# Summing the four corners of a deformable-convolution gather in a PSUM bank, beside layer 1

## The chip, the cores and the metric

One core of a Trainium2 chip runs the whole network in one launch. The metric is the time of one execution in microseconds (us). TensorE is called PE (PEld is its weight load), VectorE DVE, ScalarE ACT, GpSimd POOL, and SP issues DMAs. All data are float32.

## The reference, cut to what matters

Four layers run in sequence on an input of 8 images of 128 channels by 64 x 64; each is `x = x + layer(group_norm(x))`. Three of them matter here.

- Layer 1 propagates along rows and columns. For each of four directions (down, up, right, left), with its own 9-tap 1-D convolution over 128 channels:

```python
def step(prev, cur):
    new = cur + jax.nn.relu(_conv1d(prev, w))
    return (new, new)
_, outs = jax.lax.scan(step, xm[0], xm[1:])
```

  That is a chain of 63 dependent steps per direction, 252 in all.
- Layer 2 is a 5 x 1 convolution, a 3-tap one per channel and a gate.
- Layer 3 is a deformable convolution. An offset convolution gives each pixel and each of the 9 taps a fractional position and a mask; the sample is the weighted sum of the four corners of that position, and a matrix product over taps and channels follows:

```python
samp = corner(y0, x0, (1 - wy1) * (1 - wx1)) + corner(y0, x0 + 1, (1 - wy1) * wx1) \
     + corner(y0 + 1, x0, wy1 * (1 - wx1)) + corner(y0 + 1, x0 + 1, wy1 * wx1)
samp = samp * mask[:, None]
out = jnp.einsum('bckhw,ock->bohw', samp, dcn_w.reshape(COUT, C, KK))
```

Then a batch norm over all images, a leaky rectifier, and the residual.

## The kernel before, in words

Layer 1 keeps its state X in SBUF for four images at a time. Images 0 to 3 pass through it beside the end of layer 0. After an exchange, images 4 to 7 pass through it while layer 2 of images 0 to 3 and layer 3 of images 0 to 2 (and the first 30 ticks of image 3) run. The part of that second passage from tick 96 on is the stage of the change. One step of layer 1 (`propagate`, L930 and L937) is 9 float32 products, which the trace shows as 18 matmuls and 18 weight loads, into one PSUM tile `ps_l`; DVE then applies `X = max(ps_l, 0) + X`, and the next step reads that X.

Layer 2 and the preparation of layer 3 (`Layer2.plan`) are lists of small functions with due ticks, 96 ticks to an image: `t1_product` L1064, `t4_product` L1078, the gate in DVE L1092 to L1100, `tokens` (PE transposes L1134, copied by ACT L1137 and L1140, and stored as a table in DRAM), `offsets` L1161, `offsets_out` (ACT `omc` L1172, then transposes L1175), and the positions and weights of the gather.

Layer 3 (`Layer3`) runs one image behind. A tick handles 3 of the 9 taps for 128 pixels. What it issues at tick n:

1. `fetch`: three indirect DMAs from POOL (L1288), one per tap. Each brings, for 128 pixels, the four corners of 128 channels: 512 columns of `got`, which has 3 x 4 x 128 columns. There are `GOT` = 6 such buffers. After layer 1 has ended, X is cut into more of them.
2. The functions that earlier ticks left for this one: `sum` of tick n-1, `turn` of n-2, `keep` of n-3, and every sixth tick `convolve`, later `bias` and `store`.
3. `weigh`: DVE multiplies corners 0 to 2 of all three taps by their weights in one operation of 1152 columns (L1306), and ACT multiplies corner 3 in three activations of 128 columns (L1310).

With `sums` = 2, beside layer 1, `sum` adds the corners on DVE in two operations (L1321): corners 0 and 1 get 2 and 3 (768 columns), then corner 0 gets corner 1 (384 columns). `turn` transposes the three results on PE into a tile `ps_s` (L1328), of which a pool has three; `keep` copies it to `samp` on ACT (L1335). `convolve` (L1341) multiplies by the weights, 9 products over two pixel groups. With `sums` = 0, after layer 1, nothing is added on DVE: `turn` accumulates the four corners in PSUM with four transposes per tap, and the product's weights lie in the PSUM bank that layer 1 has left (`wps`, L1302).

The order on each engine is the program's order, written out by hand in the loop over ticks n: first the tick of layer 3 (from n = 96), then the functions of layer 2 that are due, then as many steps of layer 1 as a running balance of PE's costs allows (`load`, `pace`, `STEP`). Layer 1 ends at `last` = 414, so 318 ticks run with `sums` = 2. After it the loop interleaves the residual of images 4 to 7 (`residual`, L887 to L897), whose layer 2 comes next.

Of the kernel before, what the change touches and what calls it, by code (L numbers as in the profile page):

```python
# [10 lines left out]
F32 = mybir.dt.float32  # L11
I32 = mybir.dt.int32
AF = mybir.ActivationFunctionType
ALU = mybir.AluOpType
PSUM = bass.MemoryType.PSUM
DRAM = bass.MemoryType.DRAM

P = 128
B, C, H, W = 8, 128, 64, 64
# [4 lines left out]
T = 512  # L24
# [16 lines left out]
def conv_preact_kernel(ctx: ExitStack, tc: tile.TileContext, a: dict, out: bass.AP):  # L41
    nc = tc.nc
# [38 lines left out]
    with tc.tile_pool(name="x", bufs=1) as xp, tc.tile_pool(name="l1w", bufs=1) as wd, tc.tile_pool(  # L81
        name="l1ps", bufs=1, space=PSUM
# [16 lines left out]
        with tc.tile_pool(name="l2w", bufs=1) as wp, tc.tile_pool(name="l2", bufs=2) as w2, tc.tile_pool(  # L99
            name="l3", bufs=2  # L100
        ) as w3, tc.tile_pool(name="l2ps", bufs=2, space=PSUM) as p2, tc.tile_pool(
            name="l3ps", bufs=3, space=PSUM
        ) as p3, tc.manual_schedule():
            st2 = [const.tile([P, NCH, 6], F32, name=f"st2_{b}") for b in range(B)]
            one = propagate(tc, a, wd, pl, X)
# [20 lines left out]
            for b in range(B):  # L126
                for when, what in sorted(two.plan(b).items()):
                    n = b * two.TICKS + when
                    if b == NB2:
                        n = (b + 1) * two.TICKS - (two.TICKS - 5 - when) // 2  # L130
# [3 lines left out]
            first = two.TICKS  # L134
            load = {
                n: 2 + 18 * (n % 6 == 3) + sum(f.products for f in plans.get(n, ())) for n in range(first, last)
            }
            steps, taken, total = 4 * H, 2 * NCH - 1, 0
            for n in range(min(plans), (B + 1) * two.TICKS):
                b, i = n // two.TICKS - 1, n % two.TICKS  # L140
                if b >= 0:
                    three.tick(b, i, two.done[b], 2 if n < last else 0)
                for f in plans.pop(n, ()):
                    f()
                if n < two.TICKS:
                    if n % 3 == 0:
                        next(one)
                        taken += 1
                elif n < last:
                    if n == first:  # L150
                        pace = (sum(load.values()) + STEP * (steps - taken)) / (last - first)
                    total += load[n]
                    while total + STEP / 2 <= pace * (n + 1 - first) and taken < steps:
                        next(one)
                        taken, total = taken + 1, total + STEP
                else:
                    if n == last:
                        run(one)
                        three.bank = pl
                    if n < last + 12 or n % 3 == 0:  # L160
                        if next(late, True) and not three.more:
                            size = 3 * 4 * C
                            flat = X.rearrange("p h b -> p (h b)")
                            for i in range(HW * NB2 // size):
                                piece = flat[:, i * size : (i + 1) * size]
                                three.more.append(piece.rearrange("p (k q c) -> p k q c", k=3, c=C))
                            three.turns = 0
# [1090 lines left out]
class Layer3:  # L1258


    PAIR, G3, WT = 2, 3, 16

    def __init__(self, tc, a, ident, tables, od, st, wp, w2, pp):
        nc = self.nc = tc.nc
        self.ident, self.tables, self.od, self.st = ident, tables, od, st
        self.w2, self.pp = w2, pp
        self.dcn_w = wp.tile([P, KK, P], F32, name="dcn_w")
        nc.sync.dma_start(self.dcn_w, a["dcn_w"])
        self.dcn_b = wp.tile([P, 1], F32, name="dcn_b")
        nc.sync.dma_start(self.dcn_b, a["dcn_b"])  # L1270
        self.bank = self.wps = None
        self.more, self.turns = [], 0
        self.late = {}
        self.n = 0
# [21 lines left out]
    def weigh(self, b, t, k0, wgt, got, sums):  # L1296
        nc, G3 = self.nc, self.G3
        if k0 == 0 and t % self.WT == 0:
            self.wps = None
            if self.bank is not None:  # L1300
                self.wps = self.bank.tile([P, self.WT, KK, 3], F32, tag="ps_l1", name="wps")
                nc.scalar.copy(self.wps, wgt[:, t : t + self.WT, :, 0:3])  # L1302
        if k0 == 0 and t % self.PAIR == 0:
            self.samp = self.w2.tile([P, KK, self.PAIR * P], F32, name="samp")
        w = wgt[:, t, k0 : k0 + G3, 0:3] if self.wps is None else self.wps[:, t % self.WT, k0 : k0 + G3, :]
        nc.vector.tensor_mul(  # L1306
            got[:, :, 0:3, :], got[:, :, 0:3, :], w.unsqueeze(3).to_broadcast([P, G3, 3, C])
        )
        for k in range(G3):
            nc.scalar.activation(  # L1310
                got[:, k, 3, :], got[:, k, 3, :], AF.Identity, scale=wgt[:, t, k0 + k, 3:4]
            )
        self.later(1, self.sum, got, sums)
        self.later(2, self.turn, got, sums, self.samp, k0, t % self.PAIR * P)
        if k0 + G3 == KK and t % self.PAIR == self.PAIR - 1:
            self.later(4, self.convolve, b, t + 1 - self.PAIR, self.samp)

    def sum(self, got, sums):
        for n in range(sums):
            q = 2 - n  # L1320
            self.nc.vector.tensor_add(got[:, :, 0:q, :], got[:, :, 0:q, :], got[:, :, q : 2 * q, :])  # L1321

    def turn(self, got, sums, samp, k0, col):
        nc, parts = self.nc, 4 >> sums
        ps = self.pp.tile([P, self.G3, P], F32, name="ps_s")
        for k in range(self.G3):
            for q in range(parts):
                nc.tensor.matmul(  # L1328
                    ps[:, k, :], lhsT=got[:, k, q, :], rhs=self.ident, is_transpose=True,
                    start=(q == 0), stop=(q == parts - 1),  # L1330
                )
        self.later(1, self.keep, ps, samp, k0, col)
# [123 lines left out]
```

## Time and profile before

| what | value |
|---|---|
| median of 5 runs | 6308.25 us (6293.68 to 6322.04) |
| the profiled execution, time | 6319.36 us |
| its span | 6317.4 us |
| busy over the span | PE 83%, PEld 57%, DVE 67%, ACT 47%, POOL 69% |
| mean granted PE clock | 0.899 |
| first gather issue, last layer-1 update | 2948.08 us, 4393.52 us |
| last gather issue | 6132.5 us |

All groups, waits and chains that the text reads come from the profiled execution. A row of a group names the line, the engine, the operation, the tile written and the tiles read, the shapes and the count; then the busy time and the mean of one, and after the second bar the time the engine stood idle before them, with what ended it. In a timeline, a row gives start and duration, and in brackets the idle time before it with its releaser. "issue" is time in which the engine waited for nothing that the profile shows. Matmul ends are modelled, so a busy PE need not be at its peak. The span cut in 40 slices (each digit the busy share in tenths; the stage of the change lies in slices 19 to 28):

```profile
PE   3677877889999999889999999998888787876650
DVE  4889999888787878232877777776655454544334
ACT  4667677664554543122443444433445455554442
POOL 3777888876666666112777787777667777777765
```

### The profile page before, as it was taken

Reading aid. Unit: us, or ns where it says so; the run is one execution under the profiler, and the core shown is the slowest. Engines: PE = TensorE matmul, PEld = TensorE weight load, DVE = VectorE, ACT = ScalarE, POOL = GpSimd, SP = SyncE. Lnnn points to the kernel's source line nnn. Section 1 sums busy time; section 2 is a strip of 40 time slices with the busy share of each in tenths; the row PEclk is TensorE's granted clock in tenths of the full one; section 3 lists DMA queues with packets and bytes.
Section 4 is the critical chain, followed back from the end, with each engine's and each line's share of the span. In section 5 each row is a group of like instructions: output and inputs, shape, how many; then the busy total and the mean of one; then the engine's idle time right before and its main releaser. Section 6 shows DMA issues by size and latency. Waiting matters only on the chain.

```text
span 6317.4 us, 76412 instructions
## 1 busy us (share of the span) xinstructions
PE 5250.7 (83%) x25372; PEld 3616.2 (57%) x25372; DVE 4217.2 (67%) x4615; ACT 2999.1 (47%) x5848; POOL 4335.4 (69%) x3758
## 2 busy tenths in 40 slices
PE   3677877889999999889999999998888787876650
PEld 1122222247676767666777777787666666665550
DVE  4889999888787878232877777776655454544334
ACT  4667677664554543122443444433445455554442
POOL 3777888876666666112777787777667777777765
PEclk7777777789999999999999999999989899998885
DMA  4676676655555545233776777767788888787778
GB/s 122 194 203 188 194 201 186 182 160 149 144 148 146 151 137 145 69 136 104 214 212 198 212 205 214 215 192 203 253 274 253 248 250 250 244 258 219 216 212 292
DMA packets 516713, 1231.28 MB, mean 195 GB/s; under 512 B 79320, under 2 KB 120224, under 8 KB 514272
## 3 DMA queue, kind: packets, MB, share of 16 engines
q0 software_dynamic: 184320, 604.13, 32.8%
q1 hardware_dynamic: 320480, 597.10, 31.9%
q10 hardware_dynamic: 11520, 25.18, 1.0%
q8 instruction: 202, 3.31, 0.2%
q14 instruction: 191, 1.56, 0.1%
HBM read 1064.79 MB, written 161.32 MB: 194 GB/s over the span
## 4 chain that ended last, share of the span: by engine, by line
PE 52%; DMA 17%; DVE 6%; issue 4%; POOL 4%; ACT 3%; SPq 0%; POOLq 0%; DVEq 0%; ACTq 0%
PE ps_l L930 29%; DMA X<-table,idx 6%; DMA got<-table,idx 6%; PE ps_o L1341 5%; PE ps_s L1328 4%; PE ps_t L1064 3%; POOL got L1288 2%; PE ps_y L801 2%; PE ps_t L1078 2%; PE ps_off L1161 1%; DVE X L937 1%; DMA o_in<-od 1%; DVE hb L786 1%; DVE got L1306 1%; PE ps_x L488 1%
## 5 line engine op out<-in xcount | busy, mean ns | idle before, releaser
L1288 POOL DMA_INDIRECT got<-table,idx x1614 | 1766.7, 1095 | 774.5 <-issue 369.3
L930 PE MATMUL ps_l<-X,w_dir 128*128 128x240 f32 (+4 forms) x9072 | 2031.3, 379 | 93.7 <-DVE X L937 65.8
L930 PEld LDWEIGHTS ps_l<-X,w_dir 128*128 128x128 f32 x9072 | 1704.5, 192 | 466.2 <-DVE X L937 210.2
L792 POOL TENSOR_TENSOR hb<-hb,C 128x1024 f32<-128x1024 f32 x512 | 1209.1, 2362 | 65.3 <-DMA C<-cs 24.1
L786 DVE TENSOR_TENSOR_SCAN hb<-da,carry,ub_ps 128x512 f32<-128x512 f32 x896 | 1097.9, 1267 | 81.3 <-ACT da L769 25.1
L769 ACT ACTIVATE da<-dt_s,a_neg 128x512 f32<-128x512 f32 x1024 | 678.2, 714 | 657.0 <-DVE hb L786 604.4
L1310 ACT ACTIVATE got<-got,wgt 128x128 f32<-128x128 f32 x1614 | 587.1, 402 | 531.8 <-DMA got<-table,idx 503.4
L1288 POOL DMA_INDIRECT X<-table,idx x690 | 653.6, 947 | 210.2 <-issue 91.7
L937 DVE SCALAR_TENSOR_TENSOR X<-ps_l,X 128x256 f32<-128x256 f32 x504 | 213.3, 423 | 776.4 <-PE ps_l L930 773.9
L1328 PE MATMUL ps_s<-ident,got 128*128 128x128 f32 x3594 | 520.7, 293 | 174.1 <-ACT samp L1335 77.8
L777 DVE TENSOR_TENSOR ub_ps<-u_s,B_ps 128x1024 f32<-128x1024 f32 x512 | 625.6, 1222 | 53.7 <-DMA u_s<-ud 28.7
L1306 DVE TENSOR_TENSOR X<-X,wps 128x1152 f32<-128x1152 f32 x230 | 311.3, 1354 | 451.3 <-DMA X<-table,idx 416.0
L1328 PEld LDWEIGHTS ps_s<-ident,got 128*128 128x128 f32 x3594 | 454.6, 152 | 267.1 <-ACT samp L1335 105.7
L1341 PE MATMUL ps_o<-samp,dcn_w 128*128 128x256 f32 x2304 | 530.9, 386 | 0.0
L1306 DVE TENSOR_TENSOR got<-got,wps 128x1152 f32<-128x1152 f32 x202 | 272.6, 1351 | 359.8 <-DMA got<-table,idx 337.8
L1328 PE MATMUL ps_s<-ident,X 128*128 128x128 f32 x2760 | 380.1, 297 | 154.9 <-ACT samp L1335 94.1
L1321 DVE TENSOR_TENSOR got<-got 128x768 f32<-128x768 f32 x636 | 484.7, 762 | 25.0 <-ACT got L1310 6.7
L1341 PEld LDWEIGHTS ps_o<-samp,dcn_w 128*128 128x128 f32 x2304 | 441.8, 195 | 71.8 <-issue 14.8
L1335 ACT COPY samp<-ps_s 128x384 f32<-128x384 f32 x768 | 361.3, 471 | 234.8 <-PE ps_s L1328 234.5
L1306 DVE TENSOR_TENSOR got<-got,wgt 128x1152 f32<-128x1152 f32 x336 | 453.0, 1349 | 28.2 <-DMA got<-table,idx 28.0
L1328 PEld LDWEIGHTS ps_s<-ident,X 128*128 128x128 f32 x2760 | 346.1, 155 | 196.5 <-ACT samp L1335 108.1
L791 POOL COPY carry<-hb 128x2 f32<-128x2 f32 x512 | 95.7, 187 | 527.0 <-DVE hb L786 491.5
(219 smaller groups left out, 5796.8 us busy)
## 6 DMA issues: line engine op xcount, KB each, us to landing
dt_s<-dtd SPq DMA_DIRECT2D x512, 256.0 KB
u_s<-ud SPq DMA_DIRECT2D x512, 256.0 KB
C<-cs SPq DMA_DIRECT2D x128, 256.0 KB
table<-tok SPq DMA_DIRECT2D x128, 256.0 KB
got<-table,idx POOLq DMA_INDIRECT x1614, 3.9
x<-x2d SPq DMA_DIRECT2D x48, 384.0 KB
x3h<-x3d SPq DMA_DIRECT2D x16, 1056.0 KB
dtd<-dt SPq DMA_DIRECT2D x64, 256.0 KB
```

The costliest lines, as they stand in the source:

```text
L769: nc.scalar.activation(da[:, k], steps[i]["dt"], AF.Exp, scale=a_neg[:, q, k : k + 1])
L777: nc.vector.tensor_mul(ub, st["u"].unsqueeze(1).to_broadcast([P, 2, T]), s["B", h])
L786: nc.vector.tensor_tensor_scan(hb[:, k, :], st["da"][:, k, :], ub[:, k, :], start, ALU.mult, ALU.add)
L792: nc.gpsimd.tensor_mul(hb, hb, S[c]["C", h])
L930: nc.tensor.matmul(ps[:, c0:c1, :], lhsT=w[:, k, :], rhs=v[:, prev, c0 + k - PAD : c1 + k - PAD, :], start=(k == PAD), stop=(k == K - 1),)
L1288: nc.gpsimd.indirect_dma_start(out=got[:, k, :, :].rearrange("p q c -> p (q c)"), out_offset=None, in_=self.tables[b], in_offset=bass.Indi ...
L1306: nc.vector.tensor_mul(got[:, :, 0:3, :], got[:, :, 0:3, :], w.unsqueeze(3).to_broadcast([P, G3, 3, C]))
L1310: nc.scalar.activation(got[:, k, 3, :], got[:, k, 3, :], AF.Identity, scale=wgt[:, t, k0 + k, 3:4])
L1321: self.nc.vector.tensor_add(got[:, :, 0:q, :], got[:, :, 0:q, :], got[:, :, q : 2 * q, :])
L1328: nc.tensor.matmul(ps[:, k, :], lhsT=got[:, k, q, :], rhs=self.ident, is_transpose=True, start=(q == 0), stop=(q == parts - 1),)
L1335: self.nc.scalar.copy(samp[:, k0 : k0 + self.G3, col : col + P], ps)
L1341: nc.tensor.matmul(ps, lhsT=self.dcn_w[:, k, :], rhs=samp[:, k, :], start=(k == 0), stop=(k == KK - 1))
```

## The change

Where `sums` is set, that is beside layer 1: the weighted corner 0 goes to a PSUM bank (`banks[2]`, 384 of its 512 columns), corner 1 is weighted in place, both on DVE. ACT weighs corners 2 and 3, six activations instead of three. `sum` adds corners 1 and 2 into the bank and writes bank + corner 3 to corner 0 of `got`: three operations of 384 columns. Transposes use the two other banks in turn. The three tiles `ps_s` become three fixed banks, so PSUM holds no more than before; after layer 1 all three serve the transposes again, and the products, activations and transposes there are what they were. The instructions and the order on POOL stay as they are.

```diff
--- before.py
+++ after.py
@@ -99,7 +99,7 @@
         with tc.tile_pool(name="l2w", bufs=1) as wp, tc.tile_pool(name="l2", bufs=2) as w2, tc.tile_pool(
             name="l3", bufs=2
         ) as w3, tc.tile_pool(name="l2ps", bufs=2, space=PSUM) as p2, tc.tile_pool(
-            name="l3ps", bufs=3, space=PSUM
+            name="l3ps", bufs=1, space=PSUM
         ) as p3, tc.manual_schedule():
             st2 = [const.tile([P, NCH, 6], F32, name=f"st2_{b}") for b in range(B)]
             one = propagate(tc, a, wd, pl, X)
@@ -1268,6 +1268,7 @@
         nc.sync.dma_start(self.dcn_w, a["dcn_w"])
         self.dcn_b = wp.tile([P, 1], F32, name="dcn_b")
         nc.sync.dma_start(self.dcn_b, a["dcn_b"])
+        self.banks = [pp.tile([P, T], F32, name=f"bank{i}") for i in range(3)]
         self.bank = self.wps = None
         self.more, self.turns = [], 0
         self.late = {}
@@ -1302,27 +1303,36 @@
                 nc.scalar.copy(self.wps, wgt[:, t : t + self.WT, :, 0:3])
         if k0 == 0 and t % self.PAIR == 0:
             self.samp = self.w2.tile([P, KK, self.PAIR * P], F32, name="samp")
-        w = wgt[:, t, k0 : k0 + G3, 0:3] if self.wps is None else self.wps[:, t % self.WT, k0 : k0 + G3, :]
-        nc.vector.tensor_mul(
-            got[:, :, 0:3, :], got[:, :, 0:3, :], w.unsqueeze(3).to_broadcast([P, G3, 3, C])
-        )
-        for k in range(G3):
-            nc.scalar.activation(
-                got[:, k, 3, :], got[:, k, 3, :], AF.Identity, scale=wgt[:, t, k0 + k, 3:4]
-            )
+        w = wgt[:, t, k0 : k0 + G3, :] if self.wps is None else self.wps[:, t % self.WT, k0 : k0 + G3, :]
+        spread = lambda q0, q1: w[:, :, q0:q1].unsqueeze(3).to_broadcast([P, G3, q1 - q0, C])
+        if sums:
+            nc.vector.tensor_mul(self.total(), got[:, :, 0, :], w[:, :, 0:1].to_broadcast([P, G3, C]))
+            nc.vector.tensor_mul(got[:, :, 1:2, :], got[:, :, 1:2, :], spread(1, 2))
+        else:
+            nc.vector.tensor_mul(got[:, :, 0:3, :], got[:, :, 0:3, :], spread(0, 3))
+        for q in (2, 3) if sums else (3,):
+            for k in range(G3):
+                nc.scalar.activation(
+                    got[:, k, q, :], got[:, k, q, :], AF.Identity, scale=wgt[:, t, k0 + k, q : q + 1]
+                )
         self.later(1, self.sum, got, sums)
         self.later(2, self.turn, got, sums, self.samp, k0, t % self.PAIR * P)
         if k0 + G3 == KK and t % self.PAIR == self.PAIR - 1:
             self.later(4, self.convolve, b, t + 1 - self.PAIR, self.samp)
 
+    def total(self):
+        return self.banks[2][:, 0 : self.G3 * P].rearrange("p (k c) -> p k c", c=P)
+
     def sum(self, got, sums):
-        for n in range(sums):
-            q = 2 - n
-            self.nc.vector.tensor_add(got[:, :, 0:q, :], got[:, :, 0:q, :], got[:, :, q : 2 * q, :])
+        if sums:
+            total = self.total()
+            for q, to in ((1, total), (2, total), (3, got[:, :, 0, :])):
+                self.nc.vector.tensor_add(to, total, got[:, :, q, :])
 
     def turn(self, got, sums, samp, k0, col):
         nc, parts = self.nc, 4 >> sums
-        ps = self.pp.tile([P, self.G3, P], F32, name="ps_s")
+        ps = self.banks[self.n % (2 if self.bank is None else 3)]
+        ps = ps[:, 0 : self.G3 * P].rearrange("p (k c) -> p k c", c=P)
         for k in range(self.G3):
             for q in range(parts):
                 nc.tensor.matmul(
```

## The prediction

> **What bounds the kernel now.** I read the span in slices first, then the groups of one stretch, then the waits and the chain of work. The change touches only ticks 96 to 413 of the gather, which run beside the second half of layer 1, from about 2960 to 4394 us. The groups of instructions between 3000 and 4390 us, shapes kept apart (count, busy us, mean ns, idle before it and who ended it):
>
> ```profile
> L1288 POOL DMA_INDIRECT got<-table,idx x929 | 1097.5, 1181 | 293.3 <-issue 217.9 <-ACT got L1310 20.7 <-ACT samp L1335 19.6
> L1306 DVE TENSOR_TENSOR got<-got,wgt 128x1152 f32<-128x1152 f32 x311 | 419.7, 1350 | 28.2 <-DMA got<-table,idx 28.0
> L1310 ACT ACTIVATE got<-got,wgt 128x128 f32<-128x128 f32 x932 | 330.3, 402 | 207.7 <-DMA got<-table,idx 196.7 <-DVE got L1321 9.3 <-DVE bn_st L1357 0.3
> L1321 DVE TENSOR_TENSOR got<-got 128x768 f32<-128x768 f32 x311 | 296.2, 952 | 12.3 <-ACT got L1310 5.0
> L1321 DVE TENSOR_TENSOR got<-got 128x384 f32<-128x384 f32 x310 | 177.3, 572 | 10.7
> ```
>
> POOL is saturated: 1097.5 us of gather issues plus 293.3 us before them is the whole 1390 us, and nearly all of those gaps are the 0.30 us that stands before every issue. But PE is nearly full too. In the table of stretches (us, then PE, PEld, DVE, ACT and POOL busy, clock) the stage and the late gather read:
>
> ```profile
> 2960.00:4394.00 1434.00, 1371.33 (x6682) 1104.81 (x6680) 1079.79 (x1379) 571.54 (x1514) 1123.13 (x954) 0.99 0.70 205
> 4670.00:6140.00 1470.00, 1136.37 (x6937) 925.07 (x6936) 669.41 (x645) 720.05 (x1832) 1107.86 (x1167) 0.90 0.80 242
> ```
>
> PE is busy 96% of the stage, so a faster POOL can win only the places where PE stood still for a late gather. The timeline shows them; this is the worst (start, duration, idle before it):
>
> ```profile
> 3549.92 1.36 DVE L1306 TENSOR_TENSOR got<-got,wgt 128x1152 f32<-128x1152 f32 x1 [4.35 <-DMA got<-table,idx]
> ...
> 3552.26 7.08 PE L930 MATMUL ps_l<-X,w_dir 128*128 128x256 f32 x18 [3.64 <-DVE X L937]
> ```
>
> DVE's queue stood on a gather, the layer-1 update X behind it came late, PE waited 3.64 us, and its 18 matmuls then took 7.08 us instead of the usual 4.02.
>
> **Why an issue takes 1181 ns.** After 4800 us, where the product's weights come from PSUM, the same issue takes 947 to 948 ns. Beside layer 1 it is lengthened when it starts during a DVE operation with two SBUF inputs:
>
> ```profile
> 4373.42 1.35 DVE L1306 TENSOR_TENSOR got<-got,wgt 128x1152 f32<-128x1152 f32 x1
> 4374.04 1.55 POOL L1288 DMA_INDIRECT got<-table,idx  x1 [0.30 <-issue]
> 4375.76 0.45 PEld L1328 LDWEIGHTS ps_s<-ident,got 128*128 128x128 f32 x3
> 4375.90 0.94 POOL L1288 DMA_INDIRECT got<-table,idx  x1 [0.30 <-issue]
> ```
>
> The issue at 4374.04 starts while the product runs (to 4374.77) and needs 0.6 us more than the one at 4375.90.
>
> [...]
>
> **The change, part by part** (318 ticks of three gathers each).
>
> *DVE.* Gone per tick: 1350 + 952 + 572 = 2874 ns. Added: two products and three sums of 384 columns. An SBUF sum of 384 takes 572 ns. For PSUM operands the nearest rows are layer 2's gate, 512 columns at 685 and 687 ns; between the 384 and 768 rows (0.99 ns a column) an SBUF sum of 512 would take 699. So PSUM costs nothing extra: 558 to 572 each, 2.79 to 2.86 us, and two more gaps of 35 ns (10.7 us over 310). I take +0.04 us a tick (ends -0.08 and +0.12), 13 us on an engine that is busy 75%; it lies beside PE's matmuls, except where PE waits for a sum (below).
>
> [...]
>
> *POOL.* A tick now has 2.87 us of DVE work with two SBUF inputs; afterwards only the two products have them, 1.14 us (a sum has one input in PSUM). An issue that meets an operation at a random moment waits its remainder, so the excess goes with the sum of squares: 1.350² + 0.952² + 0.572² = 3.06 against 2 x 0.572² = 0.65. The excess of 234 ns becomes 50 ns; its ends are 0 and 234. A tick then needs 3 x (0.947 + 0.050 + 0.305) = 3.9 us of POOL, while the stage gives 1434 / 318 = 4.5. POOL runs ahead until the six buffers stop it.
>
> *ACT.* Three more weighings. Three in a row take 0.99 us, so +315 us: ACT goes from 571 to 886 us of 1434, 62%. Behind them in ACT's queue stand the samples' copy L1335 (which frees a transpose bank for PE), layer 2's copies, and `omc` L1172, for which PE waits. Hidden by: ACT's 197.7 us of waits for gathers, which go when POOL leads, and its waits for PE. The sums hide most of the delay, too: the first needs no weighing of ACT, the second only the first three, the third the last three. If ACT has finished three by time A after DVE is free, the sums ended at max(0, A) + 1.54 and now end at max(1.71, A + 1.57).
>
> *Two banks instead of three.* Transposes of a tick now wait for the copy of two ticks before. On ACT that copy stands right behind the weighings whose sums these transposes read anyway. Cost: nothing, up to 0.5 us (one copy, 474 ns) in a tick without a layer-1 step; after 4394 us there are three banks as before.
>
> **The sum.** Gains where PE waited for a late gather: at 3552 us 3.64 less the usual 0.19, plus 7.08 - 4.02, is 6.5; at 3984 us 2.31 + 1.69 = 4.0; one more wait for DVE, at 3937 us, 1.0. Together 11.5. Costs: PE's two waits of 3.6 us for `omc` (3284 and 3644 us) have two ticks' weighings in front, 2 x 2 x 0.99 = 4.0; some six waits of PE for a sum get 0.17 each, 1.0. The stage wins 6.5 us.
>
> Then the tail. At 4391 us ACT waits 1.03 us for a gather: POOL has no lead. From 4394 us the residual's reloads bound, then, from 4440 to 4480 us, the gathers again:
>
> ```profile
> by line: DMA got<-table,idx 43.6%; PE ps_s L1328 14.7%; POOL got L1288 12.9%; PE ps_o L1341 11.7%; issue 11.3%; DVE got L1306 3.4%; ACT got L1310 2.8%; POOLq L1288 0.3%; DVEq L1306 0.1%; ACT samp L1335 0.1%
> ```
>
> With a lead of two more ticks (3.75 us each there, 7.5) this stretch shrinks; some 2 us of it POOL already made up under the residual. I take 5.5. After 4480 us POOL waits up to 7.4 us for buffers, so a greater lead buys nothing. Total 6.5 + 5.5 = 12 us: the profiled execution of 6319.36 us would become 6307, and the median of 6308.25, which lies 11 us below it, **6296 us**.
>
> **Rivals.**
> 1. *POOL was the bound more widely.* The `omc` waits also go (7.2 us; ACT no longer stands on gathers before them), so do PE's waits for sums and ACT's weighings (3214, 3581, 4024 us: 4.8) and the full lead of three ticks (11) is kept: 11.5 + 7.2 + 4.8 + 11 = 34.5, so 6274. For it: POOL is full. Against: at 3284 us the `omc` wait stood behind two ticks' weighings with data in hand.
> 2. *ACT's queue takes POOL's place, slower.* Layer 2's 48 token ticks put a copy of 0.59 or 0.69 us into ACT's queue between weighings, and PE's next transposes wait for ACT's sample copy. If each shows one tick's 0.99 us, 48 x 0.99 = 47.5, less a tail of 7: +40, 6348. It decides from the point where ACT has no idle left between PE's transposes and the next copy; now ACT has 3.17 us there in a plain step, but a burst at 3280 us had none.
> 3. *The change does not do what it says*: products and PSUM sums hold POOL as before (1181 ns stays). Then only costs are left, 5 us plus about 5 us of DVE's 13 where it runs late: 6318.
>
> **How the numbers follow.** Forecast 0.43 (its own range 6284 to 6308), rival 1 0.24, rival 2 0.20, rival 3 0.13. About 0.3% (19 us: 6289.3 to 6327.2) is what a measurement here can tell from no change. Faster: all of rival 1 and 0.11 of the forecast, 0.35. Slower: nearly all of rival 2 and a little of 3, 0.20. Same: 0.45. The range reaches into rival 1 to 6264 and to rival 2's centre, 6346, leaving some 0.08 below and 0.10 above.
>
> **What would show it.** Right: gather issues beside layer 1 near 1.00 us and POOL waiting for buffers; the new DVE operations at 0.55 to 0.58 us; no 7 us group of L930 behind a gather; ACT near 62% there, without its waits for gathers; layer 1 ending about 6 us earlier. Wrong: issues still near 1.18 us; PSUM sums above 0.62 us; or PE waiting for the samples' copy or ACT in the ticks of layer 2's tokens.

## The result and the profile after

The kernel after takes 6303.99 us (median of 30 runs, 6286.32 to 6320.79) against 6311.71 us for the kernel before (56 runs, 6287.12 to 6333.57): a ratio of 0.9989, interval 0.9982 to 0.9996. The forecast was 12 us less, what came is 7.7 us less, inside the band that was called no change beforehand. The profiled execution after took 6310.94 us, span 6309.2 us, clock 0.901.

The groups between 3000 and 4390 us, the same window as before the change (count, busy us, mean ns, idle before it and its releasers):

```profile
L1289 POOL DMA_INDIRECT got<-table,idx x929 | 909.1, 979 | 484.5 <-issue 205.3 <-PE bank L1338 161.6 <-DVE X L937 41.5
...
L1315 ACT ACTIVATE got<-got,wgt 128x128 f32<-128x128 f32 x1859 | 578.0, 397 | 0.0
L1330 DVE TENSOR_TENSOR bank<-bank,got 128x384 f32<-128x384 f32 x622 | 349.6, 562 | 36.8 <-ACT got L1315 1.6 <-ACT ps_t L1088 0.5 <-DVE bank L1330 0.5
...
L1309 DVE TENSOR_TENSOR bank<-got,wgt 128x384 f32<-128x384 f32 x311 | 176.3, 567 | 10.8
L1330 DVE TENSOR_TENSOR got<-bank,got 128x384 f32<-128x384 f32 x311 | 173.6, 558 | 33.8 <-ACT got L1315 2.0 <-DVE bank L1330 0.5
L1310 DVE TENSOR_TENSOR got<-got,wgt 128x384 f32<-128x384 f32 x311 | 171.3, 551 | 0.0
```

Read the first row first: the gather's issue fell from 1181 to 979 ns, and what POOL now waits for are buffers (the transposes L1338 have to read one before it is free). The second: ACT's 207.7 us of idle time before its weighings are 0.0. The other four are the new DVE operations, all between 551 and 567 ns, with an operand in PSUM or without. The stretches (us, then PE, PEld, DVE, ACT and POOL busy, clock, DMA share and GB/s):

```profile
2960.00:4394.00 1434.00, 1373.85 (x6678) 1105.19 (x6677) 1046.52 (x2009) 823.62 (x2464) 933.43 (x955) 0.99 0.69 205
4670.00:6140.00 1470.00, 1139.42 (x6927) 926.98 (x6926) 667.12 (x641) 716.73 (x1823) 1101.25 (x1162) 0.90 0.80 242
```

POOL is relieved of 190 us in the stage, DVE of 33, and ACT has 252 us more. PE has the same 1371 to 1374 us, and the stage is not shorter: from the first gather to the last update of layer 1 it was 2948.08 to 4393.5, 1445.4 us; now it is 2950.41 to 4396.8, 1446.4 us.

Where the gain should have come from, and where it went, stands in PE's own rows. Weight loads of PE from 2960 to 4394 us (busy, mean, idle before them by releaser), before:

```profile
L930 PEld LDWEIGHTS ps_l<-X,w_dir 128*128 128x128 f32 x3731 | 700.2, 192 | 138.8 <-DVE X L937 64.9 <-issue 7.1 <-DVE got L1306 0.8
...
L1328 PEld LDWEIGHTS ps_s<-ident,got 128*128 128x128 f32 x951 | 120.1, 141 | 55.3 <-issue 15.8 <-ACT got L1310 9.4 <-ACT samp L1335 7.7
...
L1175 PEld LDWEIGHTS ps_om<-ident,omc 128*128 128x128 f32 x24 | 2.9, 154 | 8.5 <-ACT omc L1172 8.5
```

and after:

```profile
L930 PEld LDWEIGHTS ps_l<-X,w_dir 128*128 128x128 f32 x3731 | 700.2, 192 | 133.8 <-DVE X L937 59.8 <-issue 7.2 <-DVE got L1310 0.8
...
L1338 PEld LDWEIGHTS bank<-ident,got 128*128 128x128 f32 x948 | 119.6, 141 | 57.8 <-ACT got L1315 20.2 <-issue 16.3 <-DVE got L1330 1.8
...
L1175 PEld LDWEIGHTS ps_om<-ident,omc 128*128 128x128 f32 x24 | 2.9, 154 | 11.2 <-ACT omc L1172 11.2
```

The layer-1 products wait 5.0 us less, nearly all of it for X. The transposes wait 2.5 us more in all (10.8 more for ACT's weighings, less for other releasers), those of `omc` 2.7 us more. 5.0 won, 5.2 lost.

The slow groups of matmuls went the same way. The one at 3552 us that took 7.08 us is gone; its place reads 3.92 us (start, duration). But a new one stands behind the longer `omc` wait. Before the change, where that wait was 3.65 us, no slow group followed:

```profile
3283.91 0.66 PE L1175 MATMUL ps_om<-ident,omc 128*128 128x128 f32 x4 [3.65 <-ACT omc L1172]
3284.41 3.92 PE L930 MATMUL ps_l<-X,w_dir 128*128 128x256 f32 x18
```

and after it:

```profile
3290.40 1.12 PE L1175 MATMUL ps_om<-ident,omc 128*128 128x128 f32 x4 [4.47 <-ACT omc L1172]
...
3291.31 5.34 PE L930 MATMUL ps_l<-X,w_dir 128*128 128x256 f32 x18
...
3553.82 3.92 PE L930 MATMUL ps_l<-X,w_dir 128*128 128x256 f32 x18
...
3584.10 5.60 PE L930 MATMUL ps_l<-X,w_dir 128*128 128x256 f32 x18
```

The last line follows a wait of 2.28 us for ACT's weighings. Groups of L930 that took over 0.6 us more than their share of 4.02 us for 18: five before, 10.0 us over in all; five after, 9.9 us.

Beside each such group the granted clock is low. All ten overlap stretches of 3.4 or 6.8 us in which the profile's granted clock of PE is 0.50. Here is the stretch of the 7.08 us before, then that of the 5.34 us after (us, then PE, PEld, DVE, ACT and POOL busy, clock, DMA share and GB/s):

```profile
3551.70:3558.50 6.80, 6.25 (x15) 5.17 (x16) 3.19 (x5) 1.98 (x6) 5.33 (x5) 0.50 0.60 157
```

```profile
3287.40:3294.20 6.80, 3.80 (x12) 3.28 (x13) 1.35 (x3) 5.59 (x20) 4.97 (x7) 0.50 0.87 265
```

In the whole stage the clock is 0.50 for 23.9 us before and 30.7 us after. Why one wait of PE brings such a stretch (4.47 us at 3290) and another does not (3.65 us at 3284) is not shown.

So the profiled pair differs elsewhere: from the end of layer 1 to the last gather it has 1739.0 us before and 1727.5 us after. Tick by tick, the gathers of after are 3.3 us later than those of before at 4535 us (tick 448) and 6.0 us earlier at 4689 us (tick 480): the time is won between these two, not from 4440 to 4480 us as forecast. The stretch from tick 448 to 480, before and then after:

```profile
4535.20:4689.10 153.90, 129.04 (x793) 98.23 (x792) 86.86 (x108) 72.95 (x185) 94.20 (x96) 0.90 0.83 266
```

```profile
4538.50:4683.10 144.60, 121.35 (x791) 92.58 (x790) 86.66 (x108) 72.74 (x187) 93.24 (x96) 0.95 0.85 280
```

It is 9.3 us shorter, and 7.7 us of that is PE's busy time for the same matmuls, at a clock of 0.95 instead of 0.90. Whether that is the change or the execution, the experiments had to say.

### The profile page after: what moved, and what is told of

Read it like the earlier page. It is cut to its first block, busy times and chain, and to the rows that moved or that the text cites. A ratio compares the mean times of both kernels' runs of the same rounds, so it can differ in the third digit from the quotient of the medians.

```text
span 6309.2 us, 78370 instructions
## 1 busy us (share of the span) xinstructions
PE 5245.5 (83%) x25372; PEld 3614.8 (57%) x25372; DVE 4194.9 (66%) x5251; ACT 3249.8 (52%) x6802; POOL 4143.1 (66%) x3758
## 3 DMA queue, kind: packets, MB, share of 16 engines
q8 instruction: 202, 3.31, 0.2%
## 4 chain that ended last, share of the span: by engine, by line
PE 31%; DMA 14%; DVE 4%; POOL 4%; issue 3%; ACT 2%; POOLq 0%; SPq 0%; DVEq 0%; ACTq 0%
PE ps_l L930 14%; DMA X<-table,idx 6%; DMA got<-table,idx 5%; PE ps_o L1351 5%; PE bank L1338 4%; PE ps_t L1064 3%; POOL got L1289 2%; PE ps_t L1078 2%; PE ps_off L1161 1%; POOL X L1289 1%; DMA o_in<-od 1%; DVE X L937 1%; ACT got L1315 1%; PE ps_tok L1134 1%; DVE bank L1330 0%
## 5 line engine op out<-in xcount | busy, mean ns | idle before, releaser
L1289 POOL DMA_INDIRECT got<-table,idx x1614 | 1574.8, 976 | 956.3 <-issue 361.1
L930 PE MATMUL ps_l<-X,w_dir 128*128 128x240 f32 (+4 forms) x9072 | 2031.2, 379 | 89.8 <-DVE X L937 61.6
L930 PEld LDWEIGHTS ps_l<-X,w_dir 128*128 128x128 f32 x9072 | 1704.5, 192 | 462.0 <-DVE X L937 206.2
L1315 ACT ACTIVATE got<-got,wgt 128x128 f32<-128x128 f32 x2568 | 840.3, 398 | 297.2 <-DMA got<-table,idx 277.3
L937 DVE SCALAR_TENSOR_TENSOR X<-ps_l,X 128x256 f32<-128x256 f32 x504 | 213.4, 423 | 778.5 <-PE ps_l L930 776.5
L1338 PE MATMUL bank<-ident,got 128*128 128x128 f32 x3594 | 513.5, 290 | 166.3 <-ACT samp L1345 64.2
L1338 PEld LDWEIGHTS bank<-ident,got 128*128 128x128 f32 x3594 | 448.4, 150 | 257.3 <-ACT samp L1345 80.3
L1338 PE MATMUL bank<-ident,X 128*128 128x128 f32 x2760 | 384.9, 299 | 159.1 <-ACT samp L1345 91.7
L1345 ACT COPY samp<-bank 128x384 f32<-128x384 f32 x768 | 361.7, 471 | 254.3 <-PE bank L1338 253.3
L1338 PEld LDWEIGHTS bank<-ident,X 128*128 128x128 f32 x2760 | 350.3, 156 | 201.1 <-ACT samp L1345 110.2
L1315 ACT ACTIVATE X<-X,wgt 128x128 f32<-128x128 f32 x690 | 265.3, 402 | 335.1 <-DMA X<-table,idx 333.4
L1330 DVE TENSOR_TENSOR bank<-bank,got 128x384 f32<-128x384 f32 x636 | 357.5, 562 | 38.8 <-ACT got L1315 3.0
```

What stands on the lines that cost most here:

```text
L930: nc.tensor.matmul(ps[:, c0:c1, :], lhsT=w[:, k, :], rhs=v[:, prev, c0 + k - PAD : c1 + k - PAD, :], start=(k == PAD), stop=(k == K - 1),)
L1289: nc.gpsimd.indirect_dma_start(out=got[:, k, :, :].rearrange("p q c -> p (q c)"), out_offset=None, in_=self.tables[b], in_offset=bass.Indi ...
L1315: nc.scalar.activation(got[:, k, q, :], got[:, k, q, :], AF.Identity, scale=wgt[:, t, k0 + k, q : q + 1])
L1330: self.nc.vector.tensor_add(to, total, got[:, :, q, :])
L1338: nc.tensor.matmul(ps[:, k, :], lhsT=got[:, k, q, :], rhs=self.ident, is_transpose=True, start=(q == 0), stop=(q == parts - 1),)
L1345: self.nc.scalar.copy(samp[:, k0 : k0 + self.G3, col : col + P], ps)
```

## The experiments

**Theory 1**: PE's own order of work bounds the stage; relieving POOL buys little there, and ACT's weighings give back what it buys. **Theory 2**: POOL was the bound, and ACT's queue took its place. All ratios are against the kernel before on the same chip in the same set. On the chips of the first two sets and of the last run the kernel before itself takes 6721 to 6734 us, on that of the third set 6316 us; the two kinds of chip are kept apart below, because the change does something else on the first kind. The expectations of the first four runs were set for the kind of chip of the recorded pair, on which none of the four ran, so they can't be held against them.

### Parts of the change, on a chip where before takes 6734 us

*act_only* (kernel before; ACT weighs two corners, DVE's product has 768 columns, sums stay in SBUF):

```diff
+        m = 2 if sums else 3
...
-            got[:, :, 0:3, :], got[:, :, 0:3, :], w.unsqueeze(3).to_broadcast([P, G3, 3, C])
+            got[:, :, 0:m, :], got[:, :, 0:m, :], w.unsqueeze(3).to_broadcast([P, G3, m, C])
...
+        for q in range(m, 4):
```

> Only the second weighing on ACT: corners 2 and 3 on ACT, sums on DVE in SBUF in two operations as before. Theory 1: gather issues about 1.10 us, POOL still full most of the stage, ACT near 58%; the stage 3 to 8 us longer than before, no lead of POOL at its end, time 6311 to 6320. Theory 2: POOL's relief by a third (234 to about 160 ns an issue) shortens the stage by 15 us or more, time under 6300.

Measured: 6797.14 us, ratio 1.009 (1.0066 to 1.0114).

*bank_only* (kernel after, but ACT weighs corner 3 alone and DVE's second product has 768 columns):

```diff
-            nc.vector.tensor_mul(got[:, :, 1:2, :], got[:, :, 1:2, :], spread(1, 2))
+            nc.vector.tensor_mul(got[:, :, 1:3, :], got[:, :, 1:3, :], spread(1, 3))
-        for q in (2, 3) if sums else (3,):
+        for q in (3,):
```

> Only the PSUM sums: DVE weighs corners 0 to 2 (384 + 768 columns), ACT only corner 3 as before. Theory 1 (PE's own order bounds the stage beside layer 1; POOL's relief buys back only a few PE waits, and the added ACT weighings give about as much away): ACT near 40% in the stage, PE's waits for omc back to about 8 us and those for ACT's weighings to about 11 us, gather issues near 1.03 us, the stage 5 to 10 us shorter than in the changed kernel, time 6294 to 6300. Theory 2 (POOL bounded the stage, ACT's queue has taken its place): the stage at least 20 us shorter than before, time 6285 or less.

Measured: 6860.55 us, 1.0187 (1.0161 to 1.0213).

*act_three* (kernel after, but ACT weighs corners 1 to 3 and DVE one):

```diff
-            nc.vector.tensor_mul(got[:, :, 1:2, :], got[:, :, 1:2, :], spread(1, 2))
-        for q in (2, 3) if sums else (3,):
+        for q in (1, 2, 3) if sums else (3,):
```

> ACT weighs three corners (nine activations a tick), DVE one, sums in PSUM. Theory 1: POOL as in the changed kernel or faster (issues near 0.96 us), but each PE wait behind ACT's weighings grows by some 1 us; the stage 8 to 15 us longer than in the changed kernel, time 6310 to 6320. Rival (ACT's queue has slack, its cost is not in PE's waits): the same as the changed kernel within 4 us.

Measured: 6902.91 us, 1.0244 (1.0215 to 1.0273).

*less_gather* (kernel before; from the seventh tick on the third of a tick's three gathers is left out beside layer 1, so its columns hold old values; six fixed buffers):

```diff
-        for k in range(G3):
+        for k in range(G3 if self.bank is not None or self.turns <= GOT else G3 - 1):
```

> The kernel before with only two of three taps gathered per tick beside layer 1, from the seventh tick on (the third tap's corners stay those of an earlier tick). POOL needs a third less there and must run ahead. Theory 1: the stage from first gather to last layer-1 update is only 8 to 15 us shorter than the 1445 us of before, time 6285 to 6300. Theory 2: POOL was the bound, the stage is 40 us or more shorter, time under 6270.

Measured: 6640.29 us, 0.9857 (0.9828 to 0.9886).

Each part of the change costs time here, and leaving gathers out saves it, so neither theory holds on this chip as it stands: the kernel before has some 115 us in the stage that it does not have elsewhere (before_again, below), and the change adds to them. The kernels before and after themselves had to be seen under these conditions.

### Before and after themselves, on a second chip of this kind

*before_again* is the kernel before, unchanged, in one profiled execution; *after_again* the kernel after; *bank_only_2* and *act_three_2* repeat the two above. Theory 3 was added here: a POOL that runs ahead makes its gathers stand in the way of something that the engines need and that the profile doesn't name, so that relieving POOL costs time. Where the expectations speak of PE waiting for instructions, they mean the waits that the profile calls "issue"; no run shows what PE waits for there.

> The kernel before once more, for the spread of one profile against another. If the chip is like the one of the recorded pair: stage (first gather to last layer-1 update) 1445 us, PE's waits for issue below 20 us outside layer 2, no lead of POOL at the end of the stage, and gather 1201 some 1803 us after the first, give or take 5. If it is like the chip of the first four experiments: time near 6730, PE waiting some 280 us for its own instructions (issue), most of it after layer 1.

> The changed kernel on the same chip as the runs beside it. Theory 1: ratio 0.998 to 1.000 where PE does not wait for instructions. If PE does: a theory 3 is added, that a POOL that runs ahead of PE makes the gathers' transfers stand in the way of PE's instruction loading, so that what relieves POOL costs time; it expects the changed kernel 1% to 2% slower than before there, between act_only (1.009) and act_three (1.024); theory 1 expects it within 0.5% of before even there.

> Sums in PSUM, three corners weighed by DVE. Theory 1, on a chip where PE does not wait for instructions: 0.997 to 0.9995 of before, the stage 5 to 10 us shorter than in the changed kernel. Theory 3, on one where it does: slower than before by 1.5 to 2.2% again.

> ACT weighs three corners. Theory 1, where PE does not wait for instructions: the stage 8 to 15 us longer than in the changed kernel, ratio 1.000 to 1.002. Theory 3, where it does: slower by 2 to 2.8% again.

Measured: before_again 6749.75 us (before: 6733.09); after_again 6898.86, 1.0243 (1.0215 to 1.027); bank_only_2 1.0201 (1.0172 to 1.023); act_three_2 1.0257 (1.0229 to 1.0284).

Theory 1 had expected after_again within 0.5% of before even here; that failed. Theory 3 had expected 1% to 2%, 1.5% to 2.2% and 2% to 2.8%: somewhat too little for after_again, right for the other two. The waits from 2960 to 4480 us (us in all, times, longest) show what is different. before_again:

```profile
DVE X L937 <- PE ps_l L930: 199.3, 114, 7.0
...
DVE X L937 <- remote: 111.2, 18, 10.9
...
PEld ps_l L930 <- DVE X L937: 58.2, 75, 6.8
PEld ps_l L930 <- issue: 49.8, 57, 7.7
```

and after_again:

```profile
DVE X L937 <- remote: 198.3, 45, 11.0
DVE X L937 <- PE ps_l L930: 187.8, 86, 7.3
...
PEld ps_l L930 <- DVE X L937: 115.6, 85, 6.2
...
ACT samp L1345 <- remote: 115.2, 24, 6.7
```

"remote" is a releaser that the profile can't name. In the recorded pair no engine has such a wait between 2960 and 4394 us; here X has 18 of them, and 45 after the change. The name alone proves little, though: the traces of this kind of chip hold fewer records of semaphores, by which releasers are found. Up to the first gather before and before_again have 35,919 each; in the stage before has 21,786, before_again 11,515, after_again 11,309 and less_gather 12,632. So the standstills have to be read from start times. In before_again's timeline one looks like this (the profile puts X's wait down to `ps_s`, which X doesn't read):

```profile
3710.86 4.02 PE L930 MATMUL ps_l<-X,w_dir 128*128 128x256 f32 x18 [0.19 <-DVE X L937]
...
3714.72 4.05 PE L1341 MATMUL ps_o<-samp,dcn_w 128*128 128x256 f32 x18
...
3719.56 0.42 DVE L937 SCALAR_TENSOR_TENSOR X<-ps_l,X 128x256 f32<-128x256 f32 x1 [6.02 <-PE ps_s L1328]
...
3721.12 0.47 ACT L1351 ACTIVATE o_out<-ps_o,dcn_b 128x256 f32<-128x256 f32 x1 [6.79 <-remote]
```

The matmuls that X needs end at 3714.88, DVE begins X at 3719.56, 4.7 us later; ACT begins o_out 2.4 us after the end of its matmuls. The update of layer 1 is late, and the loads of layer 1's products stand still for longer: over the stage their idle time is 142.6 us in before, 186.5 in before_again and 280.7 in after_again, 94 of the 137 us by which the stage of after_again is longer than that of before_again. The loss of the change lies in the stage, from the first gather to layer 1's last update. The last column counts, from 2960 us to that update, the X that begin over 1 us after both their matmuls' end and the end of DVE's last operation:

| kernel | stage, us | DVE X <- remote, 2960 to 4480 us | X late by over 1 us |
|---|---|---|---|
| before and after (recorded) | 1445.4 and 1446.4 | none | none |
| before_again | 1560.5 | 111.2 us, 18 times | 103.8 us, 26 times |
| after_again | 1697.4 | 198.3, 45 | 203.5, 64 |
| act_only | 1618.4 | 183.4, 31 | 162.5, 43 |
| bank_only | 1685.3 | 147.5, 38 | 154.5, 58 |
| bank_only_2 | 1666.1 | 151.2, 40 | 176.6, 65 |
| act_three | 1720.3 | 217.8, 41 | 206.3, 54 |
| act_three_2 | 1717.1 | 211.0, 41 | 211.2, 57 |
| less_gather | 1452.6 | 4.5, once (2960 to 4394 us) | 8.5, 5 times |

With a third of the gathers left out, these waits are gone and the stage is nearly as short as in the recorded pair (1445.4). So gathers have to do with them; their own issue is not longer here (1171 ns in before_again against 1178 in the same stage of before). The rest of the program says the same: up to the first gather this kind of chip needs no more time (2939.2 us in before_again, 2948.1 in before), and from layer 1's end to the last gather, where less_gather too fetches all of its taps, before_again needs 2047.5 us and less_gather 2052.7, against 1739.0 in before. The granted clock of PE is lower there (0.97 from 2960 to 4480 us in before_again and 0.95 in after_again, against 0.99 in the recorded pair), but DVE and ACT stand still too, so it can't be the whole cause. Whether the recording, which loses records just there, has a part in the standstills was not tested.

### Only the added instructions; POOL as busy as before; fewer gathers

These ran on a chip where the kernel before takes 6316 us.

*before_split* (kernel before with as many instructions as after, all of DVE's in SBUF):

```diff
+        for q0, q1 in ((0, 2), (2, 3)) if sums else ((0, 3),):
...
+        for k in range(G3 if sums else 0):
+            x = wgt[:, t, k0 + k, 3:4]
+            nc.scalar.activation(self.dot[:, k : k + 1], x, AF.Identity, scale=x)
...
+        for to, q in ((0, 2), (1, 3), (0, 1)) if sums else ():
+            self.nc.vector.tensor_add(got[:, :, to, :], got[:, :, to, :], got[:, :, q, :])
```

> The kernel before, beside layer 1 alone: DVE's 1152-column product in two operations (768 + 384), its 768-column and 384-column sums as three of 384 in SBUF, and three 128x1 activations on ACT whose results nobody reads. So two more DVE and three more ACT instructions in a tick, as many as the change adds, but every DVE operation still reads and writes SBUF alone, and POOL is not relieved. On a chip on which the kernel before takes some 6310 us: theory 1 (PE's own order bounds) expects the ratio 1.000 to 1.003. On one on which it takes some 6730 us: if the number of instructions that the engines have to load makes the change's loss there, the ratio is 1.010 to 1.025 and the stage beside layer 1 grows from 1560 to over 1620 us; if the relief of POOL (or the new operations' work) makes it, 1.000 to 1.005 and under 1580 us.

Measured: 6305.74 us, 0.999 (0.9979 to 1.0002).

*after_slow_pool* (kernel after, each gather beside layer 1 followed by a write on POOL that nobody reads):

```diff
+            if self.bank is None:
+                nc.gpsimd.memset(self.dot, 0.0)
```

> The kernel after with POOL's relief taken back: beside layer 1 POOL writes a 128x128 tile of zeros that nobody reads after each gather (some 200 ns, the 203 ns by which the gathers' issue became shorter), so that POOL is as full as it was before; ACT's and DVE's work and their instructions stay those of the kernel after. On a chip on which the kernel before takes some 6730 us and the kernel after 1.024 of that: if a POOL that runs ahead makes the loss (theory 3), most of it goes: 1.000 to 1.010, stage under 1620 us; if the added instructions or the longer work of ACT and DVE make it (theory 2 or a count of instructions), it stays: 1.020 to 1.035, stage some 1700 us. On a chip on which before takes some 6310 us: theory 1 expects 1.000 to 1.004, since the 8 us gained between 4540 and 4690 us come of POOL's relief and go with it.

Measured: 6303.72 us, 0.9995 (0.9983 to 1.0007).

*after_less* (kernel after with the cut of less_gather):

> The kernel after with two of each tick's three gathers beside layer 1 left out to one: from the seventh tick on the third tap is not fetched (its columns hold old values), six fixed buffers. All operations of DVE, ACT and PE stay. Beside the kernel before with the same cut, which took 0.986 of before with a stage of 1453 us on a chip where before takes some 6730 us: if the engines' waits for nothing that the profile names come of gathers standing in the way of the loading of instructions, they go here too, whatever the number of instructions: 0.983 to 0.992, stage under 1480 us. If ACT's and DVE's longer work makes the loss of the change there, it stays beside less_gather: 1.000 to 1.015, stage over 1520 us. On a chip on which before takes some 6310 us: 0.998 to 1.000, since PE's order bounds the stage.

Measured: 6313.59 us, 1.0004 (0.9992 to 1.0017).

All three lie just outside the range that was expected on this kind of chip (1.000 to 1.003, 1.000 to 1.004, 0.998 to 1.000), each by less than its interval. The stage's row in the table of stretches, first after_slow_pool:

```profile
2960.00:4394.00 1434.00, 1367.07 (x6688) 1102.54 (x6686) 1058.43 (x2015) 830.80 (x2483) 1162.10 (x1898) 0.99 0.70 206
```

then after_less:

```profile
2960.00:4394.00 1434.00, 1373.45 (x6696) 1106.49 (x6694) 1050.57 (x2015) 823.28 (x2465) 628.50 (x646) 0.99 0.51 149
```

Look at the fifth busy time, POOL's: 1162 us against 628 us, and PE's stays at 1367 and 1373. after_slow_pool has POOL as busy as the kernel before (1123), and its stage takes 1445.2 us. Its lead is not taken back: ACT waits only 2.4 us for gathers (197.7 in the kernel before), and POOL waits 118.7 us for transposes to free a buffer. after_less has POOL free for more than half of the stage and a quarter less traffic, and its stage takes 1441.5 us. In before_split the issue takes 1138 ns and the stage 1440.7 us. PE's waits for ACT are those of the kernel after wherever ACT has the added weighings (`omc` 11.3 us in both, weighings 22.5 us in both), and 8.8 and 15.8 us in before_split. The first half of theory 1 holds on such a chip: nothing that POOL does between these ends moves the stage by more than 6 us. Its second half, that ACT's weighings give back what the relief buys, rests on the waits of the recorded pair; bank_only, made to test it, never ran on such a chip.

All five kernels on this kind of chip, one profiled execution each (us):

| kernel | first gather at | stage | layer 1's end to last gather | first to last gather | ratio |
|---|---|---|---|---|---|
| before | 2948.1 | 1445.4 | 1739.0 | 3184.4 | |
| after | 2950.4 | 1446.4 | 1727.5 | 3173.9 | 0.9989 |
| before_split | 2942.0 | 1440.7 | 1738.8 | 3179.5 | 0.999 |
| after_slow_pool | 2931.2 | 1445.2 | 1735.1 | 3180.3 | 0.9995 |
| after_less | 2951.8 | 1441.5 | 1739.1 | 3180.6 | 1.0004 |

Up to the first gather all five execute the same instructions, and it falls anywhere between 2931.2 and 2951.8 us; the time there at a granted clock of 0.50 goes from 690 to 734 us. after, after_slow_pool and after_less have the same instructions from layer 1's end on too: 1727.5, 1735.1 and 1739.1 us, and the one with the greatest lead of POOL has none of the 11.5 us. (At tick 480, counted from layer 1's end, after_less was still 6.0 us ahead of before, and after 9.3; PE's busy time for the same work up to there is anywhere between 230.0 and 236.8 us in the five.) So one profiled execution of each can't place a gain of 7 us, and nothing here shows the late lead as its cause.

### POOL as busy as before, on the first kind of chip

*after_slow_pool_2* is after_slow_pool again; on the chip of this run the kernel before takes 6721 us.

> The kernel after_slow_pool once more (the kernel after, with a write of 128x128 zeros on POOL after each gather beside layer 1, so that POOL is as full as before the change), in more rounds. Where the kernel before takes some 6730 us and the kernel after 1.024 of that: if a POOL that runs ahead makes the loss (theory 3), 1.000 to 1.010 and a stage under 1620 us; if the added instructions or the longer work of ACT and DVE make it, 1.020 to 1.035 and a stage of some 1700 us. Where before takes some 6310 us: theory 1 (PE's own order bounds the stage, POOL's relief is worth nothing there) expects the stage between 1440 and 1447 us again and the ratio within 0.9985 to 1.0002; if POOL's relief made the 0.1% that the kernel after gained, the ratio lies 0.001 above that of the kernel after, at 0.9995 to 1.001.

Measured: 6835.6 us, 1.017 (1.0149 to 1.019); stage 1657.8 us; waits from 2960 to 4480 us:

```profile
DVE X L937 <- remote: 149.1, 31, 8.5
...
PEld ps_l L930 <- DVE X L937: 78.0, 68, 6.0
```

It lies between the two cases that were set out. With POOL as busy as before, 39.6 of the 136.9 us that the stage had grown come back (1697.4 to 1657.8, profiles of two chips; the ratios, 1.0243 and 1.017, have intervals apart) and the waits of PE for X fall from 115.6 to 78.0 us. So POOL's pace is a part of the loss. The other 97 us can't be put down to what DVE and ACT do differently, because POOL still runs ahead here until the buffers stop it: it waits 243.6 us for transposes to free one (200.3 in after_again). before_split, with the same number of instructions, would tell a count of instructions from the operations themselves there, but it ran on the other kind of chip, where the waits don't arise. **This stays open.**

The page of after_again has two queues of kind "instruction", one with 202 packets and 3.31 MB, 16.4 KB a packet, the other with 208 packets and 1.70 MB, some 8 KB a packet. That the standstills are packets of instructions that land late behind gathers would fit less_gather, but the packets speak against it. If a standstill of X ended so, a packet of these two queues would end in it. One does in 5 of the 26 late X of before_again and in 9 of the 64 of after_again, where the packets' rate alone would put 6.6 and 13.8. In the standstill at 3714.88 us none ends. The cause stays open.

## Why the prediction was right, and where it was not

*Right: the price of an issue.* In the kernel before, from 3000 to 3200 and 4200 to 4394 us, 87 gathers whose issue starts during the product L1306 take 1.44 us on average (53 with 0.7 to 0.9 us of it left 1.56, 16 with 0.1 to 0.3 left 0.97) and 86 that start during a sum L1321 1.11, both operations with two inputs in SBUF; 31 that start during a DVE operation with an operand in PSUM (L937, L1094, L1100) take 0.95, as do 60 that start during none. The excess over 947 ns was to be 50 ns; it is 979 - 947 = 32 ns. A tick needs 3 x (0.979 + 0.30) = 3.84 us of POOL, 3.9 was forecast, and POOL waits for buffers. before_split tests the reasoning on its own: with products of 768 and 384 and three sums of 384 columns in SBUF the sum of squares is 0.952² + 0.551² + 3 x 0.555² = 2.13 against 3.06, so 234 ns should become 163; measured 1138 - 947 = 191, 43 of the 71 ns. A price in proportion to the time of these operations would have risen, to 258. The parts fit as well, on the other kind of chip: act_only 1073 ns (1.10 us was expected), bank_only 1037 (1.03), act_three 960 (0.96). less_gather does not: with the DVE work of before and two issues a tick it has 1248, so an issue does not always meet these operations at random moments. All this also settles rival 3: with the sums in a PSUM bank the issue takes 979 ns, with as many operations in SBUF (one product 384 columns longer) 1138.

*Right: DVE and PSUM.* 0.551 to 0.567 us an operation; a tick has 0.567 + 0.551 + 2 x 0.562 + 0.558 = 2.80 us against 2.87. The gaps grew by more than the two of 35 ns: without the waits for gathers and ACT they are 0.06 us a tick before and 0.25 after. Together that is +0.11 us, just inside the range of -0.08 to +0.12 (I took +0.04; the rows that the forecast names reach from -0.08 to +0.06, and no run shows where the part up to +0.12 comes from).

*Right: ACT and rival 2's point of decision.* ACT is busy 823.6 of 1434 us, 57% for a forecast of 62% (three weighings took 1.06 us of a tick before, when waits parted some of them, and six in a row take 1.86: +0.80, not +0.99). Its waits for gathers are gone. No 48 x 0.99 us arose on such a chip.

*Wrong: "The stage wins 6.5 us."* It won nothing; layer 1 ended 3.3 us later, not 6 earlier. The waits were near: 6.8 us of waits for late gathers were to go, 5.0 went; 5.0 us were to come, 5.2 came. What was mis-sized is the other term, the slow group of 18 matmuls that follows a wait. I counted it where a wait goes (7.08 - 4.02 at 3552 us and 1.69 at 3984 us, 4.75 us) and not where one comes: behind `omc` at 3291 us (+1.3) and behind ACT's weighings at 3584 us (+1.6). Two groups that were slow before became slower by 0.9 and 0.7 us, and the total of such excess stayed, 10.0 to 9.9 us. These groups lie in the stretches at a clock of 0.50, which I had not considered: I took the slow work as a part of a wait for a gather, and at 3291 and 3584 us it followed a wait for ACT. Among the waits the phrase that failed is "some six waits of PE for a sum get 0.17 each, 1.0": PE's waits for ACT's weighings grew from 9.4 to 20.2 us, and only because other waits of the same transposes shrank did 2.5 us of that remain.

*Not shown: "With a lead of two more ticks ... I take 5.5."* The gathers leave the chain, as was said, and up to tick 448 nothing is won: it comes 141.7 us after layer 1's end before and after the change. The chain from 4440 to 4480 us after the change:

```profile
by line: PE bank L1338 34.6%; issue 17.0%; DMA got<-table,idx 16.7%; PE ps_o L1351 13.2%; POOL got L1289 11.2%; ACT got L1315 6.0%; DVE got L1312 3.4%; PE gn_ps L947 1.5%; PE gn_ps L953 1.5%; ACT samp L1345 1.3%; DVE gn_mv L945 0.7%; DVE gn
```

The gathers' 43.6% became 16.7%; the transposes, 14.7%, became 34.6%. What was late next was PE's own transposes, and I had not named it. Of the 9.3 us that came between ticks 448 and 480, 7.7 are PE's shorter busy time at a higher clock. after_less, with a greater lead still, needs 1739.1 us from layer 1's end to the last gather, as the kernel before does.

*Right for no reason shown: the size.* -12 us was forecast, -7.7 us (median against median) measured, yet neither term of the sum is found where I put it, so that the forecast came near is luck. The kernel after and the three others of its chip kind lie between 0.9989 and 1.0004 with intervals that overlap; what makes the 0.11% is not settled.

*Rival 1* (6274) fell: POOL full or half idle, the stage takes 1441 to 1446 us. *Rival 2* (6348) has the right sign on the other kind of chip (+2.4%), but ACT's queue is not the main cause there: act_only, with ACT's weighings alone, costs 0.9% and bank_only, without them, 1.9 to 2.0%. Most of what PE loses stands before layer 1's products (94 of 137 us); its transposes' waits for ACT's weighings are 31.6 us in after_again, 14.9 in before_again.

## What to carry to other kernels

POOL, full in this stage, was not its bound, since PE was busy 96% of it: with 190 us less of POOL the stage took 1446.4 us instead of 1445.4. Price the relief of a full engine only by the waits of the one that is nearly full, and put the same price, the slow work after a wait included, on each wait that the change adds. Read the granted clock beside every group that is slow. Here the faster POOL only changed whose name stands in the chain (from 4440 to 4480 us the gathers fell from 43.6% to 16.7%, the transposes rose from 14.7% to 34.6%). Before a few microseconds are put down to a place in a profile, look how far the same instructions move between executions: here 20 us up to the first gather.

## What the runs showed of the hardware that was not expected

- On three chips the kernel before takes 6721 to 6734 us, and on the one of them where the whole change ran it costs 2.4%; elsewhere the same pair gives 0.9989. The time is lost from the first gather on. X, the update on DVE, begins late there (26 times in before_again, by up to 6.8 us, 103.8 us in all), and hardly ever with a third of the gathers left out (5 times, 8.5 us).
- Each part of the change costs time there although ACT and DVE have idle time (act_only: +58 us of stage for three activations more and a product 384 columns shorter in each of 318 ticks). Whether the operations do it or the shorter issue of the gathers (1073 ns) is not separated.
- In ten groups of the recorded pair the 18 matmuls of a layer-1 step took 4.9 to 7.1 us instead of 4.02, where the granted clock was 0.50 for 3.4 or 6.8 us. They stand behind waits of PE of 2.1 to 4.5 us; behind one of 3.65 us (3284 us, before) stood no slow group.
- By what DVE reads, on the chips where before takes 6308 to 6316 us, the issue of a gather took 979 ns beside sums with one PSUM operand, 1138 beside short sums in SBUF, 1181 beside long ones, and 947 to 948 after 4800 us, where no sums run and the product reads one operand in PSUM.
